# GRU and top-2 mixture on one core: GpSimd sums the last chunk's four blocks, in buffers that the slabs held

## The chip, the cores and the metric

The kernel runs on one core of a Trainium2 chip. The metric is device time in microseconds of one execution, taken as the median over several runs. A profile of one execution goes with it. The engines are named as the profile names them: PE (matrix multiply), DVE (vector), ACT (scalar), POOL (GpSimd) and SP (here only an issuer of DMAs).

## The reference

The input `x` has 16 sequences of 256 steps with 512 features, all float32. A GRU runs over the steps from the state `cond_2048`. Each of its 4096 hidden rows then goes through a mixture of eight low-rank experts, of which the router takes the best two, and the result is added to `x`.

```python
def cell(h, x):
    gi = x @ W_ih + b_ih
    gh = h @ W_hh + b_hh
    ...
    n = jnp.tanh(i_n + r * h_n)
    h_new = (1.0 - z) * n + z * h
...
router_logits = x / norm @ router_w
routing_weights = jax.nn.softmax(router_logits.astype(jnp.float32), axis=-1)
rw, selected_experts = jax.lax.top_k(routing_weights, TOP_K)
rw = rw / jnp.sum(rw, axis=-1, keepdims=True)
...
for e in range(N_EXPERTS):
    out = out + combine[:, e, None] * (x @ Wa[e] @ Wb[e])
...
x = x + _L0_ffn_ref(_L0_cond_ref(cond_2048, x, ...), ...)
```

In the mixture, `x` stands for the GRU's hidden rows.

## The kernel before

The GRU is sequential, so the 256 steps set the length of the program. They are grouped into 32 blocks of eight steps; one block is 128 rows (16 sequences by 8 steps), which is one row for each partition. The mixture's work is put between the steps, while the GRU goes on.

The first 29 blocks go through the mixture in four chunks of 7, 11, 7 and 4 blocks (`CHUNKS`, L24). For each chunk, `Route` finds the two experts of each row. `Chunk` then gives each row two slots in a list that is sorted by expert, and scatters the rows to it in DRAM. `Slab` takes the list 128 rows at a time: it loads them (tile `xg`), copies one expert's two matrices into tiles of its own (`wag` and `wbg`, by POOL, L677 and L681), multiplies, and stores the result `y` to the DRAM buffer `y_slots` (L722). When a chunk's last slab is done, one `Combine` is begun for each block:

- `load` issues the load of the block's `x` rows on SP (`xr`, L746) and two indirect DMAs on POOL, which gather the first and the second expert's rows from `y_slots` (`yg`, L750).
- `add(0)` and `add(1)` each do `xr = y * w + xr` in one DVE instruction over 128 rows and 512 columns (L764); `w` is a column with one weight per row.
- After `add(1)`, SP issues the store of `xr` to the output (L768).

The last three blocks (29, 30 and 31) are too late for a chunk. `Moe` sends each of them through all eight experts, weighted by the combine weights. `prep` and `route` make the logits. `soft1` to `soft3` make the weights: the norm on POOL (L815), then on DVE the softmax and `top2`, which begins with a small memset by POOL (tile `pr`, L307) that DVE's maximum (L312) needs. Then PE multiplies by the first matrices (L833), DVE scales by the weights (`a`, L845), PE transposes (L854), ACT copies back (L860), and PE multiplies by the second matrices (L870). `load` fetches the block's `x` rows on SP (L797), `store` adds PE's result to them on DVE (L880), and SP issues the store of the block (L881).

A planner in the Python program sets the order. Each of these objects is an agent with a list of `Piece`s. After each GRU step, and in a loop behind the last step, `choose` walks through the agents by rank and takes every piece whose gap has passed and whose buffers (`takes`, counted in `room`) are free. The two tile names "xr" and "yg" have three and two buffers; "xg" and "wg" have four each. Combines have rank 8 and stand ahead of the last block's `Moe`, which has rank 41. What is picked in a round is written to the engines in that order, and `keep_order` at the end holds each engine to the order in which its instructions were written. So SP, which issues almost all DMAs, issues them strictly in that order, and waits at one whose data are not ready.

In the last stage, behind the last GRU step, the remaining work is: the last slabs of the last chunk, the four combines of that chunk (they are called A, B, C and D below, in their order), and `Moe` of blocks 30 and 31.

Of the kernel before, what the change touches and what calls it, by code (L numbers as in the profile page):

```python
# [8 lines left out]
FP = mybir.dt.float32  # L9
# [8 lines left out]
ALU = mybir.AluOpType  # L18
# [3 lines left out]
P = 128  # L22
TS = 8
CHUNKS = [7, 11, 7, 4]  # L24
# [20 lines left out]
def gru_moe_kernel(  # L45
# [47 lines left out]
    pe, dve, act, pool, sp = nc.tensor, nc.vector, nc.scalar, nc.gpsimd, nc.sync  # L93
    B, T, D = x.shape
    E, _, R = wa.shape
# [13 lines left out]
    slb = ctx.enter_context(tc.tile_pool(name="slb", bufs=4))  # L109
# [6 lines left out]
    moe = ctx.enter_context(tc.tile_pool(name="moe", bufs=2))  # L116
# [29 lines left out]
    for side, src in enumerate((b_ih, b_hh)):  # L146
        for g in (0, 2, 1):
            tag = ("xg", "wbg")[side]
# [173 lines left out]
    class Piece:  # L322
# [4 lines left out]
        def __init__(self, gap=1, cost=0.0, pe=(), then=(), takes="", gives=""):  # L327
            self.gap, self.cost = gap, cost
            self.pe, self.then = list(pe), list(then)
            self.takes, self.gives = takes.split(), gives.split()  # L330
# [16 lines left out]
    class Early:  # L347
# [5 lines left out]
        def load(self):  # L353
            m = self.m
            if self.x is not None:
                return
            self.x = slb.tile([P, D], FP, tag="yg1", bufs=2, name=f"xe_{m}")
            for j in range(NJ):
                for s in range(2):
                    p0 = 32 * j + 16 * s  # L360
                    sp.dma_start(
                        self.x[p0 : p0 + B, 0:P],
                        x[:, 2 * m + s, j * P : (j + 1) * P],
                    )
# [40 lines left out]
        def plan(self):  # L405
            pieces = [
                Piece(then=[("load",)], takes="early"),
                Piece(gap=2, then=[("turn",)], takes="at"),
            ] + [
                Piece(gap=0, cost=c, pe=[("into", what, q)])  # L410
                for what, c in (("rn", 0.43), ("z", 0.22))
                for q in range(NQ)
            ] + [Piece(then=[("store",)], gives="early")]
            pieces[2].gap, pieces[2].takes = 1, ["ps"]
            pieces[9].then, pieces[9].gives = [("keep",)], ["ps", "at"]
            return pieces
# [320 lines left out]
    class Combine:  # L737


        def __init__(self, i, chunk, k):  # L740
            self.i, self.chunk, self.k = i, chunk, k

        def load(self):
            i, ch = self.i, self.chunk
            self.xr = moe.tile([P, D], FP, tag="xr", bufs=3, name=f"xr_{i}")
            sp.dma_start(self.xr, x[:, i * TS : (i + 1) * TS, :])  # L746
            self.y = []
            for n, ix in enumerate(ch.idx):
                y = slb.tile([P, D], FP, tag=f"yg{n}", bufs=2, name=f"yg_{i}_{n}")
                pool.indirect_dma_start(  # L750
                    out=y[:, :],
                    out_offset=None,
                    in_=ch.y[:, :],
                    in_offset=bass.IndirectOffsetOnAxis(
                        ap=ix[:, self.k : self.k + 1], axis=0
                    ),
                    bounds_check=ch.n_slabs * P - 1,
                    oob_is_err=False,
                )
                self.y.append(y)  # L760

        def add(self, n):
            i, k, o = self.i, self.k, self.xr
            dve.scalar_tensor_tensor(  # L764
                o, self.y[n], self.chunk.w[n][:, k : k + 1], o, ALU.mult, ALU.add
            )
            if n:
                sp.dma_start(out[:, i * TS : (i + 1) * TS, :], o)  # L768

        def plan(self):  # L770
            return [
                Piece(then=[("load",)], takes="xr yg"),
                Piece(gap=3, then=[("add", 0)], takes="turn", gives="turn"),
                Piece(then=[("add", 1)], takes="turn", gives="turn xr yg"),
            ]


# [230 lines left out]
    room = dict(ROOM)  # L1008
# [104 lines left out]
    for i in range(NB):  # L1113
# [26 lines left out]
        if i < n_sparse:  # L1140
            ch = chunks[-1]
            k = i - (ends[ch.c] // TS - ch.k)
# [55 lines left out]
```

## Time and profile before

| | us |
|---|---|
| median of three runs | 1357.65 |
| lowest and highest | 1355.23, 1357.68 |
| the profiled execution, its own time | 1356.92 |
| its span, first to last instruction | 1355.1 |
| PE busy | 1292.5 (95% of the span) |
| DVE busy | 736.2 (54%) |
| ACT busy | 392.1 (29%) |
| POOL busy | 284.4 (21%) |

The granted TensorE clock was 0.994 over the span. How to read the rows: a row of a group gives the line of the program, the engine, the operation, the tiles it writes and reads, the shape, how often it ran, its busy time in total and the mean time of one, and what ended the idle time before it. A row of the timeline gives the start, the duration, and then the same; in square brackets stands the idle time before it and who ended it. "SPq" is SP's queue: such a row is the issue of a DMA, not its transfer. In the chain of waits, a row "DMA" is the time from an issue to the point where the data had landed.

### The profile page before, as it was taken

What the parts mean: (1) busy time and instruction counts of PE and PEld (TensorE: products, weight loads), DVE (VectorE), ACT (ScalarE), POOL (GpSimd) and SP (SyncE); (2) the same over time, 40 slices, a digit from 0 to 9 for tenths busy, and PEclk for the clock granted to TensorE, in tenths of its full rate; (3) what the DMA queues carried; (4) which work ended last, traced back from release to release, by engine and by line L of the source; (5) the groups of instructions that cost most, each with busy time, mean ns of one, the idle gap of its engine ahead of it and who ended that gap; (6) DMA issues with size and microseconds to landing.
All of it is one profiled execution on the core that took longest, in us unless ns stands there. A gap on an engine that the chain in (4) does not pass through costs nothing. (4 is left out here: it accounts for less than half of the span.)

```text
span 1355.1 us, 68450 instructions
## 1 busy us (share of the span) xinstructions
PE 1292.5 (95%) x30378; PEld 929.7 (69%) x30378; DVE 736.2 (54%) x2678; ACT 392.1 (29%) x1354; POOL 284.4 (21%) x504
## 2 busy tenths in 40 slices
PE   6899999999999999999999999999998999989996
PEld 3577777776677777777776677777766787768752
DVE  1455555555455555555555456555565555665543
ACT  1223222322233333233332233333332333323220
POOL 2000000102221000000003323221133033353452
PEclk8999999999999999999999999999999999999998
DMA  8532322223322111122124535553345345664685
GB/s 200 143 122 97 99 91 90 91 61 130 95 72 61 55 56 56 41 59 57 50 65 132 182 90 158 151 148 101 95 142 167 103 135 168 174 199 129 199 253 167
DMA packets 149477, 158.67 MB, mean 117 GB/s; under 512 B 22646, under 2 KB 103606, under 8 KB 149180
## 3 DMA queue, kind: packets, MB, share of 16 engines
q1 hardware_dynamic: 139760, 123.83, 31.1%
q0 software_dynamic: 9280, 30.42, 7.1%
q8 instruction: 238, 3.90, 1.2%
q14 instruction: 59, 0.48, 0.1%
q10 hardware_dynamic: 140, 0.05, 0.0%
HBM read 84.21 MB, written 69.99 MB: 114 GB/s over the span
## 5 line engine op out<-in xcount | busy, mean ns | idle before, releaser
L921 PE MATMUL rn<-whh,hist 128*32 128x256 f32 x8160 | 507.8, 381 | 19.9 <-DVE hist L966 14.1
L921 PEld LDWEIGHTS rn<-whh,hist 128*32 128x32 f32 x8160 | 264.0, 109 | 198.5 <-DVE hist L966 48.3
L269 PE MATMUL rn<-wih,xT 128*32 128x256 f32 x3712 | 307.3, 382 | 9.3 <-DMA wih<-in_L_cond_W_ih_dram 5.5
L931 PE MATMUL z<-whh,hist 128*32 128x128 f32 x8160 | 289.9, 273 | 6.4 <-issue 5.8
L954 DVE SCALAR_TENSOR_TENSOR n<-r,rn 128x128 f32<-128x128 f32 x256 | 73.5, 287 | 397.6 <-ACT r L947 393.0
L931 PEld LDWEIGHTS z<-whh,hist 128*32 128x32 f32 x8160 | 247.3, 110 | 51.7 <-issue 13.5
L277 PE MATMUL z<-wih,xT 128*32 128x128 f32 x3712 | 209.0, 274 | 5.5 <-ACT z L952 3.3
L947 ACT ACTIVATE r<-rn 128x128 f32<-128x128 f32 x256 | 70.9, 277 | 460.7 <-PE rn L921 448.8
L277 PEld LDWEIGHTS z<-wih,xT 128*32 128x32 f32 x3712 | 138.5, 110 | 77.3 <-issue 6.3
L269 PEld LDWEIGHTS rn<-wih,xT 128*32 128x32 f32 x3712 | 126.7, 110 | 19.0 <-issue 13.1
L959 DVE SCALAR_TENSOR_TENSOR zh<-z,h 128x128 f32<-128x128 f32 x255 | 77.8, 305 | 86.0 <-ACT z L952 83.1
L952 ACT ACTIVATE z<-z 128x128 f32<-128x128 f32 x256 | 71.0, 277 | 170.7 <-PE z L931 144.7
L698 PE MATMUL at_ps<-xgT,wag 128*32 128x128 f32 x2752 | 110.1, 273 | 3.9 <-issue 3.5
L629 POOL TENSOR_TENSOR nrm<-ss,half 128x1 f32<-128x1 f32 x29 | 16.2, 559 | 435.5 <-ACT ht L627 408.2
L713 PE MATMUL y_ps<-wbg,at 128*32 128x256 f32 x1376 | 103.2, 380 | 1.0 <-issue 0.9
L698 PEld LDWEIGHTS at_ps<-xgT,wag 128*32 128x32 f32 x2752 | 87.6, 110 | 13.9 <-issue 10.2
L966 DVE STREAM_TRANSPOSE hist<-rows 128x128 f32<-128x128 f32 x256 | 79.7, 311 | 8.7
L974 DVE STREAM_TRANSPOSE h<-hist 128x128 f32<-128x128 f32 x256 | 79.7, 311 | 8.7
L681 POOL COPY wbg<-wb_sb 128x512 f32 x86 | 56.3, 655 | 126.0 <-PE y_ps L713 125.9
L963 DVE SCALAR_TENSOR_TENSOR rows<-zh,m 128x128 f32<-128x128 f32 x256 | 75.9, 297 | 8.9
L721 ACT COPY y<-y_ps 128x512 f32<-128x512 f32 x86 | 50.1, 583 | 101.9 <-PE y_ps L713 88.3
L961 DVE SCALAR_TENSOR_TENSOR m<-z,n 128x128 f32<-128x128 f32 x256 | 77.7, 303 | 2.4 <-ACT n L956 1.4
(136 smaller groups left out, 1072.4 us busy)
## 6 DMA issues: line engine op xcount, KB each, us to landing
xg<-x_slots SPq DMA_DIRECT2D x344, 64.0 KB
y_slots<-y SPq DMA_DIRECT2D x86, 256.0 KB
ht<-H SPq DMA_DIRECT2D x58, 256.0 KB
x_slots<-zero SPq DMA_DIRECT2D x50, 256.0 KB
x<-in_x_dram SPq DMA_DIRECT2D x256, 32.0 KB
xr<-in_x_dram SPq DMA_DIRECT2D x32, 256.0 KB
out_dram<-xr SPq DMA_DIRECT2D x32, 256.0 KB
H<-rows SPq DMA_DIRECT2D x232, 32.0 KB
```

Of the source, the lines that this page charges most:

```text
L269: pe.matmul(rn[32 * j : 32 * j + 32, 0 : 3 * P].rearrange("p (g d) -> p g d", g=3)[:, 0:3:2, :], lhsT=xts[m][:, q, :], rhs=w[:, 0:3:2, j, ...
L277: ins = pe.matmul(zb[32 * j : 32 * j + 32, 0:P], lhsT=xts[m][:, q, :], rhs=w[:, 1, j, :], start=False, stop=(q == NQ - 1), skip_group_chec ...
L698: pe.matmul(self.ps[c32, 0:P], lhsT=self.wa[:, q, c32], rhs=self.xt[:, q, :], start=(q == 0), stop=(q == NQ - 1),)
L713: pe.matmul(self.ps[c32, half], lhsT=self.at[:, c32], rhs=self.wb[:, half], start=True, stop=True,)
L921: pe.matmul(rn[32 * j : 32 * j + 32, 0 : 2 * P].rearrange("p (g d) -> p g d", g=2), lhsT=hT[:, q, :], rhs=w(q, j)[:, 0:3:2, :], start=Fals ...
L931: pe.matmul(zb[32 * j : 32 * j + 32, 0:P], lhsT=hT[:, q, :], rhs=w(q, j)[:, 1, :], start=False, stop=(q == NQ - 1), skip_group_check=True,)
L954: dve.scalar_tensor_tensor(n, r, 1.0, rn[:, P : 2 * P], ALU.add, ALU.mult)
L959: dve.scalar_tensor_tensor(zh, z, 1.0, hrow, ALU.add, ALU.mult)
L961: dve.scalar_tensor_tensor(m, z, 1.0, n, ALU.subtract, ALU.mult)
L963: dve.scalar_tensor_tensor(hn, zh, 0.5, m, ALU.mult, ALU.subtract)
L966: dve.transpose(hist[:, t, :, lo : lo + 32], hn.rearrange("p (q c) -> p q c", q=NQ))
L974: dve.transpose(hrow.rearrange("p (q c) -> p q c", q=NQ), hT)
```

## The change

For the last chunk alone (`self.last`), `Combine` changes in three ways. The `x` rows of its four blocks are loaded into buffers of the tile name "xg" and the gathered rows into buffers of "wag" and "wbg". These have four buffers each, and the slabs are through with them by then; so the plan takes and gives room "xg wg" in place of "xr yg". And the sum is done by POOL, in two instructions in place of one: a multiplication of the gathered rows by the weight column, in place, and an addition to the `x` rows.

```diff
         def load(self):
             i, ch = self.i, self.chunk
-            self.xr = moe.tile([P, D], FP, tag="xr", bufs=3, name=f"xr_{i}")
+            if self.last:
+                self.xr = slb.tile([P, D], FP, tag="xg", name=f"xr_{i}")
+            else:
+                self.xr = moe.tile([P, D], FP, tag="xr", bufs=3, name=f"xr_{i}")
             sp.dma_start(self.xr, x[:, i * TS : (i + 1) * TS, :])
             self.y = []
             for n, ix in enumerate(ch.idx):
-                y = slb.tile([P, D], FP, tag=f"yg{n}", bufs=2, name=f"yg_{i}_{n}")
+                tag, bufs = (("wag", "wbg")[n], 4) if self.last else (f"yg{n}", 2)
+                y = slb.tile([P, D], FP, tag=tag, bufs=bufs, name=f"yg_{i}_{n}")
                 pool.indirect_dma_start(
...
         def add(self, n):
             i, k, o = self.i, self.k, self.xr
-            dve.scalar_tensor_tensor(
-                o, self.y[n], self.chunk.w[n][:, k : k + 1], o, ALU.mult, ALU.add
-            )
+
+            if self.last:
+                w = self.chunk.w[n][:, k : k + 1]
+                pool.tensor_scalar_mul(self.y[n], self.y[n], w)
+                pool.tensor_add(o, o, self.y[n])
+            else:
+                dve.scalar_tensor_tensor(
+                    o, self.y[n], self.chunk.w[n][:, k : k + 1], o, ALU.mult, ALU.add
+                )
             if n:
                 sp.dma_start(out[:, i * TS : (i + 1) * TS, :], o)
 
         def plan(self):
+            room = "xg wg" if self.last else "xr yg"
             return [
-                Piece(then=[("load",)], takes="xr yg"),
+                Piece(then=[("load",)], takes=room),
                 Piece(gap=3, then=[("add", 0)], takes="turn", gives="turn"),
-                Piece(then=[("add", 1)], takes="turn", gives="turn xr yg"),
+                Piece(then=[("add", 1)], takes="turn", gives=f"turn {room}"),
             ]
```

`self.last` is set in `__init__` to `chunk.c == len(CHUNKS) - 1`.

More of the change, by code (lines that the diff above doesn't have):

```diff
@@ L741, in __init__ @@
             self.i, self.chunk, self.k = i, chunk, k
+            self.last = chunk.c == len(CHUNKS) - 1
         def load(self):
             i, ch = self.i, self.chunk
-            self.xr = moe.tile([P, D], FP, tag="xr", bufs=3, name=f"xr_{i}")
+            if self.last:
+                self.xr = slb.tile([P, D], FP, tag="xg", name=f"xr_{i}")
+            else:
+                self.xr = moe.tile([P, D], FP, tag="xr", bufs=3, name=f"xr_{i}")
             sp.dma_start(self.xr, x[:, i * TS : (i + 1) * TS, :])
```

## The prediction

> **What bounds the kernel now.** The page comes first: PE is busy 95% of the span, because the GRU runs to the last step. But the change touches only the last chunk's combines, and these run after the GRU. So what counts is the stage behind the last step, and there the table of stages shows another picture. Its columns are: window, length, then busy time of PE, weight loads, DVE, ACT and POOL, the granted clock, DMA share and GB/s.
>
> ```profile
> 1330.00:1340.00 10.00, 9.80 (x92) 3.81 (x88) 6.34 (x21) 1.57 (x4) 3.82 (x6) 1.00 0.49 145
> 1340.00:1350.00 10.00, 5.11 (x48) 1.30 (x40) 2.94 (x5) 0.00 (x0) 0.90 (x1) 0.91 0.60 170
> 1350.00:1356.00 6.00, 0.00 (x0) 0.00 (x0) 0.58 (x1) 0.00 (x0) 0.00 (x0) 0.50 0.42 124
> ```
>
> PE is through at 1345.1, and in the last fifteen microseconds no engine is busy for most of the time. The chain of waits says what is:
>
> ```profile
> 1338.08 5.29 DMA out_dram<-xr
> ...
> 1343.39 4.27 DMA xr<-in_x_dram
> ...
> 1347.78 0.06 DVE xr L880
> ...
> 1349.83 0.75 DVE xr L764
> ```
>
> Read it backward. The last DVE sum ends at 1350.58, and the span ends 4.52 us later (1355.1): that is the last store and the end of the program. Ahead of it DVE works off a pile (L880, then three L764) that all began when the x rows of block 31 landed at 1347.66. Their load (L797) was issued only at 1343.39, as its buffer, one of three "xr", came free when a combine's store had landed. PE's result had been ready since 1345.1. So the bound is the supply of "xr" buffers and SP's order, and the span has about 2.7 us (1347.8 less 1345.1) of waiting past PE in it.
>
> That waiting is all that freeing buffers could win. The timeline of POOL, over the same stretch, is where the new work goes:
>
> ```profile
> 1323.47 1.07 POOL L750 DMA_INDIRECT yg<-y_slots,ihi  x1 [2.41 <-DMA y_slots<-y]
> ...
> 1327.46 1.00 POOL L750 DMA_INDIRECT yg<-y_slots,ilo  x1 [0.30 <-issue]
> 1330.17 0.57 POOL L815 TENSOR_TENSOR nrm<-lg,half 128x1 f32<-128x1 f32 x1 [1.71 <-DVE lg L813]
> 1330.71 0.09 POOL L307 MEMSET pr<- 128x6 f32 x1
> 1332.78 1.04 POOL L750 DMA_INDIRECT yg<-y_slots,ihi  x1 [1.97 <-DVE rs L309]
> ```
>
> **What the change moves.** The two programs, laid side by side, issue the same instructions in the same order on PE and ACT, and on all engines up to the first combine of the last chunk. The differences are these. DVE loses its last eight L764. SP's last ten issues change from
>
> ```
> before: store 30, load B, store A, store B, load C, load D, load 31, store 31, store C, store D
> after:  store 30, load B, load C, load D, store A, store B, store C, store D, load 31, store 31
> ```
>
> (L881, L746, L768, L797 by their names above). POOL's order becomes: gathers A and B, norm (L815), gathers C, multiply and add of A's first half, gathers D, memset (L307), then seven more pairs of multiply and add. So three things happen: load 31 gets a free buffer, but stands behind all four combine stores; each of those waits for POOL; and the memset that block 31's top-2 needs stands behind four gathers and one pair.
>
> **The price of a pair.** The add is two-input, 128x512. The nearest rows on POOL, with counts and means:
>
> ```profile
> L681 POOL COPY wbg<-wb_sb 128x512 f32 x86 | 56.3, 655 | 126.0 <-PE y_ps L713 125.9
> L393 POOL TENSOR_TENSOR ge<-ge,bias 128x256 f32<-128x256 f32 x12 | 8.8, 732 | 0.0
> L392 POOL TENSOR_TENSOR ge<-ge,bias 128x128 f32<-128x128 f32 x12 | 5.5, 458 | 78.1 <-ACT ge L389 77.8
> L792 POOL TENSOR_TENSOR sq<-hc 128x512 f32<-128x512 f32 x3 | 3.2, 1059 | 2.4 <-issue 2.2
> ```
>
> L792 has the size but reads one tile twice: 1.06 us. L392 and L393 are true in-place adds of two tiles: 0.274 us more for 128 more columns, so 0.73 + 2 x 0.274 = 1.28 us at 512. The Trainium skill ("GPSIMD Engine Reference", section 3.1, Elementwise — side-by-side cycle accounting) states about 2.6 cycles per element for a two-input operation; at its 1.2 GHz an estimate from that page is 512 x 2.6 / 1.2 = 1.11 us before dispatch. I take 1.2. Eight adds by the row of L792 or by the extrapolation differ by 8 x 0.22 = 1.8 us, which goes into the range.
>
> The multiply by a weight column is one-input. The trace has no such operation on POOL. From below it is a copy of the size, 0.655 us (L681); from above the two-input price, 1.28. The same page (section 4.1, Engine selection) says one-input operations run at roughly line rate, and speaks against moving two-input ones from VectorE at all. I take 0.70, near the copy, as a copy too is one-input. The add reads what the multiply wrote and waits for its semaphore, which no row on POOL shows apart; POOL's independent rows follow one another with none of it, so from 0 to 0.2, and I take 0.1. A pair is 0.70 + 0.1 + 1.2 = 2.0 us. DVE needed 0.75 (L764).
>
> **The sum on POOL**, in the profiled execution's own time. Up to the norm nothing changes: it ends at 1330.74. Gathers C need no freed buffer: two issues with a period of 1.30 (1324.85 to 1326.16 above), from 1330.95 to 1333.3. Pair A-first to 1335.3; its gathers were issued at 1323.5, and DVE used the same data at 1331.74 before. Gathers D to 1337.8, memset to 1337.95. Seven pairs, 14.0: POOL ends at 1352.0. The later gathers are at least 8 us ahead of their pairs, so their landing costs nothing. I charge nothing for POOL and DVE disturbing each other: DVE has nothing to do from about 1340.5 (the second L845) until L880.
>
> **The sum behind it.** Store D is issued at 1352.05 and takes SP's usual 0.6. Load 31 goes out at 1352.7. For its landing the chain has 4.27, with loads C and D and a gather still moving. At the end of the span SP issued the last store at 1350.58 and saw it landed at 1353.25 (after a wait of 2.1): 2.7 us behind two other stores. The Trainium skill ("DMA: Bandwidth & Descriptors", section Anatomy of one DMA — SWDGE path) fits 2.0 us plus bytes over 436 GB/s, for 256 KB an estimate of 2.6. Here one store runs beside the load; I take 3.0 (between ends of 2.6 and 4.27): landed at 1355.7. With 4.27 the end would come 1.3 later. Then L880 needs 0.12 + 0.69, to 1356.5, and the 4.5 us from the last DVE sum to the end are as before: **1361.0**, which is 5.9 us past 1355.1. The freed buffer wins nothing, as it was buffer and queue together that held the load: taking away the one, the other holds it 9.3 us longer (1352.7 against 1343.39).
>
> **What stays covered.** The late memset moves DVE's L312 from 1332.94 to 1338.0. From L312 to the end of the weights is 1.12 us, then L845 to 1339.9, and 1.44 from the first transpose to L870, which runs 7.07: PE ends at 1348.5 instead of 1345.1. That is 3.4 us later, hidden by the load that lands at 1355.7; were that load early, it would be the next bound. The eight L764 taken off DVE (6 us) win nothing for the same reason; what of them was on the path is the three behind L880, some 2.1 us, already counted in that L880 is now the last.
>
> **The time.** The profiled execution took 1356.92; plus 5.9 is 1362.8. The runs shown have their median 0.7 above it (1357.65), which gives 1363.5. I say 1363.2. About 0.2% (2.7 us) is what a measurement of this kernel can tell from no change.
>
> **Rivals.**
>
> 1. The multiply on POOL costs like the two-input rows or more (1.28 us, from the upper bound), adds 1.28: a pair is 2.66 us, POOL ends 8 x 0.66 = 5.3 us later, and the time is 1368.5. For it: a weight column has to be fetched per partition. Against: the copy's row, and the rule of one input. Chance 0.2.
> 2. Not slower: POOL is quick enough that load 31 no longer decides. Then the late memset does, and PE ends at 1348.5, L880 at 1349.3, the span at 1353.8, that is 1355.6 in time (1.3 faster, within 0.2%). It decides if the load lands by 1348.5, so if POOL is through by about 1344.8: seven pairs in 6.8 us, under 1.0 each. Against it: L792's 1.06 alone is more than that. Chance 0.04, with 0.01 in it for a gain past 0.2%.
> 3. The change doesn't reorder SP as said, or load 31 is issued ahead of the stores: the same time as in 2, and no more than 0.01, as the order on the queue is fixed in the program.
> 4. Cheap pairs all the same (0.65 + 1.06, no gap: 1.71) and a landing of 2.6: POOL ends 2.3 earlier, the load 0.4: 1360.5. Chance 0.2. The likeliest case, about 1361.5 to 1365.5, has 0.55.
>
> The range, 1360.0 to 1368.3, takes in cases 1 (most of it) and 4. Faster 0.01 (out of 2), same 0.04 (the rest of 2, and 3), slower 0.95.
>
> **What would show it.** In the profile after, the chain of waits should end in: POOL's adds, store D's issue, DMA of `xr` from the input, DVE L880's sum, DMA to the output. SP should show one load (L797's line) after four stores. POOL's groups should have eight multiplies near 0.7 us and eight adds near 1.2. L312 should start near 1338, and PE should end near 1348.5, some 7 us ahead of the last DVE sum. I am wrong if a POOL pair is below 1 us, or if PE's last result ends later than the load lands.

## The result, and the profile after

The changed kernel is slower: 1372.9 us (median of six runs, 1370.1 to 1375.5) against 1356.8 for the kernel before (six runs). The ratio is 1.011, with a 95% interval of 1.0098 to 1.0122. That is 16.1 us more, where 5.9 were forecast; 1372.9 lies above the range, which ended at 1368.3. The profiled execution took 1372.6, with a span of 1370.8.

Times of whole executions drift by several microseconds, and seven experiments (the last seven rows of the table of tails) ran on a second chip, where the kernel before has its median at 1302, about 4% lower. So each ratio is against executions of the kernel before on the same chip, and for the mechanism one length is used that is free of the GRU: the **tail**, from the start of block 31's norm (L815 before, L828 after) to the end of the span, in one profiled execution of each kernel. Before it is 1355.1 - 1330.2 = 24.9 us, after 1370.8 - 1330.6 = 40.2. No tail of these two kernels was taken on the second chip. POOL's multiplies and adds cost the same there (1.56 to 1.58 and 1.26 to 1.27 us in the run with the memset early), so tails are compared across the chips.

The table of stages after, with the columns as before (length, busy time of PE, weight loads, DVE, ACT, POOL, granted clock, DMA share, GB/s):

```profile
1330.00:1340.00 10.00, 7.07 (x84) 2.39 (x69) 1.51 (x8) 0.39 (x2) 6.66 (x7) 0.99 0.59 181
1340.00:1350.00 10.00, 6.98 (x48) 3.00 (x52) 2.29 (x9) 1.17 (x2) 9.74 (x9) 0.66 0.29 80
1350.00:1360.00 10.00, 2.86 (x28) 0.61 (x20) 0.00 (x0) 0.00 (x0) 9.70 (x7) 0.85 0.20 52
```

POOL, nearly idle behind 1340 in the kernel before, is now busy from 1340 to 1360 almost without a break, and once PE is through (1352.9) no other engine is, until DVE's last sum at 1365.5. The chain of waits, from its end:

```profile
1357.14 1.26 POOL xr L774
1358.41 1.54 POOL yg L773
...
1361.32 0.54 SPq L780
...
1361.91 3.49 DMA xr<-in_x_dram
...
1365.53 0.69 DVE xr L893
```

It is the forecast's chain, link for link: POOL's last pair (its add, for which the chain has a row of POOL's queue in the place of the dots, runs from 1360.03 to 1361.29), the issue of store D, only then load 31, its landing, DVE's last sum. SP's rows show the queue: the four stores as one row of 17.9 us, in which SP does little but wait, and the load behind them.

```profile
1343.95 17.90 SPq L780 DMA_DIRECT2D out_dram<-xr  x4
1361.91 0.59 SPq L810 DMA_DIRECT2D xr<-in_x_dram  x1
```

What was mis-sized is in POOL's groups (busy time in total, mean of one in ns):

```profile
L774 POOL TENSOR_TENSOR xr<-xr,yg 128x512 f32<-128x512 f32 x8 | 10.1, 1266 | 0.7
L773 POOL TENSOR_SCALAR yg<-yg,whi 128x512 f32<-128x512 f32 x4 | 6.3, 1569 | 0.0
L773 POOL TENSOR_SCALAR yg<-yg,wlo 128x512 f32<-128x512 f32 x4 | 6.3, 1569 | 0.0
```

The add costs 1.27 us, near the 1.2 that was taken. The one-input multiply costs 1.57 us, where 0.70 was taken: it is dearer than the two-input add.

### The profile page after: what moved, and what is told of

It reads as the page before. It is cut to its first block, busy times and chain, and to the rows that moved or that the text cites. A ratio compares the mean times of both kernels' runs of the same rounds, so it can differ in the third digit from the quotient of the medians.

```text
span 1370.8 us, 68447 instructions
## 1 busy us (share of the span) xinstructions
PE 1291.9 (94%) x30378; PEld 934.7 (68%) x30378; DVE 729.6 (53%) x2670; ACT 392.7 (29%) x1354; POOL 308.3 (22%) x520
## 4 chain that ended last, share of the span: by engine, by line
PE 84%; DVE 4%; DMA 3%; issue 2%; another core or an unknown queue 2%; POOL 2%; ACT 2%; SPq 0%; POOLq 0%; ACTq 0%; DVEq 0%
PE rn L934 33%; PE z L944 16%; PE rn L269 13%; PE z L277 6%; PE y_ps L713 5%; PE at_ps L698 5%; PE gi L377 2%; DMA whh<-in_L_cond_W_hh_dram 1%; PE a_ps L846 1%; PE rt L341 1%; POOL yg L773 1%; DVE m L974 1%; DMA wih<-in_L_cond_W_ih_dram 1%; DVE rows L976 1%
## 5 line engine op out<-in xcount | busy, mean ns | idle before, releaser
L969 ACT ACTIVATE n<-n 128x128 f32<-128x128 f32 x256 | 77.3, 302 | 4.1 <-DVE n L968 3.5
```

Source lines behind the costliest of these rows:

```text
L969: act.activation(n, n, AF.Tanh)
```

## The experiments

All are made from the changed kernel unless said otherwise. The tails of all runs come first (us); "more than before" is the difference of the medians, for scale.

| kernel | tail | ratio to before, 95% interval | more than before |
|---|---|---|---|
| before | 24.9 | 1 | |
| changed kernel | 40.2 | 1.011 (1.0098 to 1.0122) | +16.1 |
| load 31 ahead of the stores | 36.0 | 1.0088 (1.0058 to 1.0118) | +11.7 |
| buffers alone, sum on DVE | 26.1 | 1.0023 (1.0006 to 1.0040) | +2.5 |
| POOL alone, old buffers | 34.6 | 1.0073 (1.0054 to 1.0092) | +9.3 |
| ACT multiplies, POOL adds | 29.4 | 1.0028 (1.0010 to 1.0045) | +4.4 |
| POOL multiplies by a number | 39.7 | 1.0132 (1.0092 to 1.0172) | +16.1 |
| POOL multiplies two-input | 35.6 | 1.0068 (1.0035 to 1.0102) | +8.9 |
| memset early | 40.1 | 1.0112 (1.0074 to 1.0149) | +13.9 |
| one more gather | 41.0 | 1.0142 (1.0121 to 1.0162) | +18.7 |
| buffers, DVE, load 31 early | 27.2 | 1.0006 (0.9994 to 1.0017) | +1.5 |
| buffers, DVE, memset early | 22.3 | 0.9974 (0.9963 to 0.9984) | -3.4 |
| buffers, DVE, both early | 21.3 | 0.9975 (0.9959 to 0.9992) | -4.9 |

**Load 31 ahead of the stores.**

```diff
-            pieces[14].then, pieces[14].takes = [("load",)], ["xr"]
+            k = 4 if self.i == NB - 1 else 14
+            pieces[k].then, pieces[k].takes = [("load",)] + pieces[k].then, pieces[k].takes + ["xr"]
```

> As the changed kernel, but the x rows of block 31 are loaded ahead of the four combine stores on SP; nothing else moves. Theory (POOL's rate and SP's order together): POOL still ends its last add at 1361.3 of the span, but only the last store follows it, so the 5 us of load and sum behind it go: span about 1365.9, time about 1368 (changed kernel 1372.9, before 1356.8). Rival 1 (PE was made late by the memset and its clock fell to 0.66, and that sets the end): no gain, about 1373. Rival 2 (the queue is the whole cause): back to before, about 1357.

Measured: the span is 1367.4 with the norm 0.85 later than in the changed kernel, so the tail is 36.0: 4.2 us won. The expectation, counted the same way, was 1365.9 - 1330.6 = 35.3. So PE's lateness (rival 1) does not set the end. Nor is the queue the whole cause (rival 2): with load 31 out of it the kernel still ends 11 us later than before, on POOL's last add.

**The buffers alone.**

```diff
-                pool.tensor_scalar_mul(self.y[n], self.y[n], w)
-                pool.tensor_add(o, o, self.y[n])
+                dve.scalar_tensor_tensor(o, self.y[n], w, o, ALU.mult, ALU.add)
```

> The buffers of the changed kernel, but the sum on DVE in one instruction as before; SP's order as in the changed kernel (four stores, then load 31). Theory (POOL's slow pair is the cause, the buffers and the queue cost nothing by themselves): gathers C and D end near 1338, the memset behind them, so DVE's sums end near 1345.5, load 31 is issued at 1346 and lands at 1349.6: span about 1355, time within 2 us of before. Rival (the queue order costs by itself): the load is held as long as in the changed kernel, over 1362. Rival (the freed buffers win their 2.7 us): about 1354.

Measured: span 1354.9, tail 26.1. So 14.1 of the 15.3 us that the tail grew come from POOL's sum, the queue that it holds up included. But the reason given for the span was wrong in one link. DVE's rows, then PE's:

```profile
1342.97 0.75 DVE L773 SCALAR_TENSOR_TENSOR xr<-yg,wlo,xr 128x512 f32<-128x512 f32 x1
1349.57 0.69 DVE L892 TENSOR_TENSOR xr<-o_ps,xr 128x512 f32<-128x512 f32 x1 [5.85 <-PE o_ps L882]
```

```profile
1338.29 0.65 PE L866 MATMUL aT_ps<-ident,a 128*128 128x128 f32 x4 [3.04 <-DVE a L857]
1340.21 1.12 PE L866 MATMUL aT_ps<-ident,a 128*128 128x128 f32 x4 [1.27 <-DVE a L857]
1341.26 8.23 PE L882 MATMUL o_ps<-wb_sb,aT 128*32 128x512 f32 x64
```

The last sum waits for PE, not for load 31. PE is late by the memset that stands behind the gathers, and then it is slow: its last 64 matmuls take 8.23 us, where they took 7.07 in the kernel before. The runs with the memset or the load moved, below, take this apart.

**POOL alone, in the old buffers.** The three uses of `self.last` that choose buffers and room are taken back; the sum stays on POOL.

> The sum on POOL as in the changed kernel, but in the buffers of before (three xr, two and two yg). SP's order becomes: stores A and B, loads C, D and 31, store 31, stores C and D. Theory: seven of eight pairs at 2.9 us still run one after another with gathers C and D between them, POOL ends near 1360, and the last thing is store D: span about 1364.5, time about 1366.5, so 6 us less than the changed kernel although it has fewer buffers. Rival (the buffers help POOL's sum, by earlier gathers): slower than the changed kernel, over 1374.

Measured: span 1363.7, tail 34.6, so 5.6 us shorter than the changed kernel's. The freed buffers do not help POOL's sum; they cost. With the old ones, the loads C, D and 31 go out after store B and ahead of stores C and D, and load 31 is at 1344.3:

```profile
1335.58 6.39 SPq L780 DMA_DIRECT2D out_dram<-xr  x2
1342.06 1.23 SPq L751 DMA_DIRECT2D xr<-in_x_dram  x2
1344.30 0.54 SPq L810 DMA_DIRECT2D xr<-in_x_dram  x1
1351.64 0.59 SPq L894 DMA_DIRECT2D out_dram<-xr  x1
1353.38 6.30 SPq L780 DMA_DIRECT2D out_dram<-xr  x2
```

With the new ones nothing in the planner holds the four stores back, and they go ahead of it. The load's place alone is 4.2 of the 5.6 us, as the run with load 31 moved shows.

**ACT multiplies.**

```diff
-                pool.tensor_scalar_mul(self.y[n], self.y[n], w)
+                act.mul(self.y[n], self.y[n], w)
```

> As the changed kernel, but ACT multiplies by the weight column (8 instructions, 0.59 us each by ACT's copies of the size) and POOL only adds. Theory (the end follows POOL's time one for one, through load 31): eight multiplies of 1.57 us leave POOL, it ends near 1348.5, load 31 goes out at 1349.1, span about 1358, time about 1360. Rival 1 (PE's delay sets the end): no change, 1373. Rival 2 (ACT's own order holds the adds up, as its copies for block 31 wait for PE among the multiplies): between 1363 and 1370.

Measured: span 1360.8, where 1358 was expected, tail 29.4, time 4.4 us over before. The end follows POOL's time, but rival 2 took 2.2 us of it (and ACT's multiply took 0.71, not 0.59): ACT's copies for block 31 stand among its multiplies and wait for PE, so POOL's adds pause.

```profile
1340.10 5.06 POOL L774 TENSOR_TENSOR xr<-xr,yg 128x512 f32<-128x512 f32 x4
1347.37 3.86 POOL L774 TENSOR_TENSOR xr<-xr,yg 128x512 f32<-128x512 f32 x3 [2.21 <-ACT yg L773]
```

**What makes the multiply dear.** Two runs replace it on POOL. One multiplies by a number and leaves the weights out, so that its output is not the reference's; the other uses a two-input multiplication with the column repeated:

```diff
-                pool.tensor_scalar_mul(self.y[n], self.y[n], w)
+                pool.tensor_scalar_mul(self.y[n], self.y[n], 0.5)
```

> As the changed kernel, but POOL multiplies the gathered rows by the number 0.5 in place of the weight column (the weights are left out). Theory A (the weight column, an operand fetched per partition, makes the multiply dear): it falls from 1.57 us to about a copy's 0.65, POOL ends 8 x 0.92 = 7.4 us earlier, span about 1363.5. Theory B (the operation itself costs 1.57 us on POOL): no change, span about 1370.8.

```diff
-                pool.tensor_scalar_mul(self.y[n], self.y[n], w)
+                pool.tensor_tensor(
+                    self.y[n], self.y[n], w.broadcast_to([P, D]), ALU.mult
+                )
```

> As the changed kernel, but POOL's multiply is written as a two-input operation, the weight column repeated over the 512 columns. If the two-input price holds (1.27 us, as the add): POOL ends 8 x 0.3 = 2.4 us earlier, span about 1368.5. If a repeated column costs as much as the operation with a scalar column: 1.57 us, span about 1370.8.

POOL's groups, the first from the run with a number, the other two from the two-input run:

```profile
L773 POOL TENSOR_SCALAR yg<-yg 128x512 f32<-128x512 f32 x8 | 12.0, 1497 | 0.0
```

```profile
L776 POOL TENSOR_TENSOR xr<-xr,yg 128x512 f32<-128x512 f32 x8 | 10.1, 1267 | 0.6
L773 POOL TENSOR_TENSOR yg<-yg,whi 128x512 f32<-128x512 f32 x4 | 4.2, 1043 | 0.0
L773 POOL TENSOR_TENSOR yg<-yg,wlo 128x512 f32<-128x512 f32 x4 | 4.2, 1040 | 0.0
```

The column accounts for 0.07 us; the operation itself costs 1.50. Theory B holds. Why it is so dear, no run shows. The same product as a two-input operation costs 1.04, less than either expectation had: like the square of one tile in the kernel before (1.06), not like an add of two tiles (1.27). The tail shrinks by 4.6, of which 8 x 0.53 = 4.2 is the multiply: the price of this one operation does move the end.

**The memset early.** For block 31 it is issued in `soft1`, behind the norm, in place of `top2`.

> As the changed kernel, but the memset that block 31's top-2 needs is issued right behind the norm, ahead of gathers C. Theory (the memset's lateness is covered by POOL's sums): PE ends 7 us earlier, near 1346, with its matmuls back at 7.1 us in all, and the time stays at that of the changed kernel within 1.5 us. Rival (PE's lateness is what costs): about 7 us less, near 1366.

Measured: tail 40.1 against 40.2, though PE ends 14.9 us after the norm's start and not 22.3. The ratio, 1.0112, is that of the changed kernel. So PE's lateness is covered, as the prediction had it. PE's rows, here and then in the changed kernel:

```profile
1280.33 7.07 PE L888 MATMUL o_ps<-wb_sb,aT 128*32 128x512 f32 x64
```

```profile
1343.02 1.97 PE L867 MATMUL aT_ps<-ident,a 128*128 128x128 f32 x8 [5.95 <-DVE a L858]
1344.92 7.94 PE L883 MATMUL o_ps<-wb_sb,aT 128*32 128x512 f32 x64
```

**Buffers and DVE, with the memset, the load, or both moved.** Each is made from the buffers-alone kernel with one or both of the edits above.

> Buffers of the changed kernel, the sum on DVE, load 31 ahead of the four stores, the memset still behind gathers C and D. The tail is counted from the start of block 31's norm to the end of the span: 24.9 us before, 26.1 with buffers and DVE alone, 21.3 with memset and load moved as well. Theory (with the sum on DVE, the late memset holds PE and PE's end decides): moving the load alone wins nothing, tail 26 us. Rival (the load behind the stores decides): 21 to 23 us.

> Buffers of the changed kernel, the sum on DVE, the memset right behind the norm, load 31 still behind the four stores. Theory: DVE's last sum comes 13 us after the norm's start, the load goes out at 13.6, its rows land at 17.2, and 0.8 + 4.5 follow: tail 22.5 us, most of what both moves won. Rival (the load behind the stores decides as much as in the changed kernel): 25 us or more.

> The buffers of the changed kernel, the sum on DVE as before, the memset behind the norm, and load 31 ahead of the four stores. Theory: nothing is left in front of PE's end at 1345 (in before's own time), L880's sum runs at once, and the span ends 0.8 + 4.5 later, near 1350.5: 4.5 us less than before, which is 0.3%. Rival (one of the three is not the bound any more and something else takes its place, as the sums of C and D ahead of L880 on DVE waiting for gathers): within 1.5 us of before.

Measured tails: 27.2 with the load alone, 22.3 with the memset alone, 21.3 with both, each within 1.2 us of what was expected (26, 22.5, and 1350.5 - 1330.2 = 20.3). The memset's place is worth 27.2 - 21.3 = 5.9 us with the load early. Of these, 2.3 are PE's last 64 matmuls, which take 9.36 us with the memset late and 7.07 with it early; most of the rest is the later start. The load's place is worth 1.0 (22.3 - 21.3), and only once the memset is out of the way: with the memset late, the tail is longer by 1.1 with the load early (27.2 against 26.1), which is again PE's last matmuls (9.36 against 8.23). The version with both is 3.6 us shorter in its tail than the kernel before; its ratio is 0.9975 (0.9959 to 0.9992), that of the memset alone 0.9974 (0.9963 to 0.9984). So these two are quicker than the kernel before, by a quarter of a percent: little, but neither interval reaches 1. In the chain of the version with both, what is left is PE's work and the sum behind it:

```profile
1276.71 7.05 PE o_ps L887 x64
1283.76 0.02 issue
1283.78 0.69 DVE xr L897
```

**The late gather.** In the changed kernel the second gather of C waits 2 us:

```profile
1331.34 1.04 POOL L756 DMA_INDIRECT yg<-y_slots,ihi  x1 [0.19 <-issue]
1334.37 1.02 POOL L756 DMA_INDIRECT yg<-y_slots,ilo  x1 [1.99 <-DMA xr<-in_x_dram]
```

The name of a load in the brackets is an inference of the profile; the data that this gather needs had long been there. The edit issues the second gather of the first chunk's first block twice.

> As the changed kernel, with one gather of the first chunk issued twice, so one more indirect DMA some 800 us ahead of the tail. In the changed kernel and in those made from it the second gather of C starts some 2 us late; it is the sixth of the last chunk and the 114th indirect DMA of the program. Theory 1 (it is the count: something happens at the 114th): the late one is now the first gather of C, the fifth of the chunk, and the sixth follows at the usual 0.3. Theory 2 (it is the number in flight in this stage): still the sixth.

```profile
1280.20 1.05 POOL L757 DMA_INDIRECT yg<-y_slots,ihi  x1 [2.72 <-issue]
1281.56 1.01 POOL L757 DMA_INDIRECT yg<-y_slots,ilo  x1 [0.30 <-DMA xr<-in_x_dram]
```

With one more gather long before, the wait moves one gather forward: it goes with the count of indirect DMAs since the program's start, at the 114th, and not with the number in flight in this stage. What happens at that count, no run shows. The second row's bracket shows again how little the named DMA means: the 0.30 there is the usual distance.

## Why the prediction was right or wrong

**Direction and mechanism: right.** Load 31 behind four stores, each behind POOL; the load's landing, DVE's last sum and the last store behind that. The chain after shows it, and moving the load alone takes 4.2 us out of the tail.

**Size: wrong, by the multiply on POOL.** It was taken at 0.70 us and measured 1.57. The forecast's tail was 1361.0 - 1330.2 = 30.8 us; measured 40.2. The 9.4 us between them are made up so:

| term | forecast | measured | difference |
|---|---|---|---|
| eight pairs | 8 x 2.0 | 8 x 2.89 (start to start) | 7.1 |
| gathers C, from the norm's end | 2.56 | 4.24 | 1.7 |
| load 31, issue to DVE's start | 3.1 | 3.6 | 0.5 |
| the rest | | | 0.1 |

- *The multiply's price* is the step that failed: 8 x 0.87 = 7.0 us of the missing 9.4. It was bounded from below by a copy (0.655) and from above by the two-input price (1.28), and taken near the copy as the row with one input. Both ends were of other operations. An operation with a scalar on POOL is a kind of its own here: 1.50 to 1.57 us, outside the bounds. The Trainium skill ("GPSIMD Engine Reference", section 4.1, Engine selection) has one-input operations at roughly line rate; the trace's copy (0.655) fits that, its multiply (1.57) doesn't, and the measurement decides. Rival 1 had the direction right, but with 1.28 as its price it stopped at 1368.5.
- *The add's price* was right within 0.07: the extrapolation from the adds of two tiles (1.28) meets 1.27, and the square (1.06), which reads one tile twice, misleads. The Trainium skill's 2.6 cycles per element ("GPSIMD Engine Reference", section 3.1, Elementwise — side-by-side cycle accounting) is not what was low: from 128 to 256 columns the adds of two tiles rise by 0.274 us, by our estimate 2.6 cycles at that page's 1.2 GHz, and from 256 to 512 by 0.534, which is 2.5. What 1.11 leaves out is a fixed part, by the same rows about 0.18 us (0.458 - 0.274); 1.2 had room for 0.09.
- *The wait of the add for the multiply* (0.1) was right: the add starts 1.65 us after the multiply does, which ends at 1.57.
- *Gathers C*: the period of 1.30 was right for seven of eight. The late one was there before too, at 1337.25, though its buffer had come free when DVE's sum ended at 1335.51; I read "issue" in its bracket as no cause and passed over it.
- *The landing*: 3.49 where 3.0 was taken, inside the bounds (2.6 to 4.27). The lower bound was the page's fit for DMAs that GpSimd issues; load 31 is issued by SP, so the fit was not made for it.
- *What stays covered* was right: PE late, no cost, as the run with the memset early shows. PE's end came later than said (1352.9, not 1348.5): 3.1 us because the memset itself was late, 1.3 us because its transposes and matmuls took longer after the idle stretch, which was not in the sum (0.5 and 0.9 us).
- *The sentence that the freed buffers win nothing* holds for the changed kernel, and says too little: with POOL's sum they cost 5.6 us (40.2 against 34.6), and with DVE's sum and the memset's place put right they win 2.6 us (24.9 against 22.3), or 3.6 with the load early too.

**The time on record**: tail 9.4 us longer, and the rest of the 9.7 us (1372.9 against 1363.2) is the base.

## What to carry to other kernels

An operation without a row in the trace is not bounded by its neighbours: a scalar multiply on GpSimd cost more than both the copy and the add that were to enclose it, so a range on such a term has to reach well past the rows, above all when it is multiplied by eight. When an agent's buffers are freed, look at what its own waits had kept back in a shared queue: here the old buffers held two slow stores behind a load that the end depended on. And look for the small instruction that a block of work is put in front of: a memset of 0.1 us behind four gathers was worth 5.9 us, once the cover was gone, and 2.3 of these were PE's slower matmuls after the pause.

## What the runs showed of the hardware

- **Some DVE instructions are held by POOL's two-input operations, and were not by its scalar ones.** Two small DVE instructions (L318, L319) ran at their usual length in the changed kernel, beside a POOL multiply. Where POOL was adding (ACT multiplies), they ended with POOL's adds. First the changed kernel, then the run with ACT:

```profile
1341.74 0.16 DVE L318 TENSOR_SCALAR mask_b<-rp 128x8 f32<-128x8 f32 x1
1341.94 0.23 DVE L319 SCALAR_TENSOR_TENSOR cb_b<-pr,s,mask_b 128x8 f32<-128x8 f32 x1
```

```profile
1340.88 1.76 DVE L318 TENSOR_SCALAR mask_b<-rp 128x8 f32<-128x8 f32 x1
1342.67 1.29 DVE L319 SCALAR_TENSOR_TENSOR cb_b<-pr,s,mask_b 128x8 f32<-128x8 f32 x1
```

  Not every DVE instruction is held: L312 to L317, beside the first of these adds, kept their lengths (0.09 to 0.20 us). In the run with POOL alone, a DVE instruction of 0.23 us (L310) took 1.22 and ended with POOL's add. The Trainium skill ("SBUF — State Buffer", section Who interferes with whom) has a read port that the two engines share and one holds for a whole instruction; the stretched rows fit that, and the multiply that stretches nothing is not in it. The prediction charged nothing for this, and the trace before could have warned: a sum on DVE that began 0.24 us after POOL's square took 1.41 us and not 0.75.

```profile
1319.96 1.10 POOL L792 TENSOR_TENSOR sq<-hc 128x512 f32<-128x512 f32 x1 [2.19 <-issue]
1320.20 1.41 DVE L764 SCALAR_TENSOR_TENSOR xr<-yg,wlo,xr 128x512 f32<-128x512 f32 x1
```

  For the changed kernel the zero was right, in part by luck: L318 and L319 happened to lie beside a multiply. Had they been held, PE's end would have come some 2.7 us later by the rows above, and still well ahead of load 31's landing (1352.9 against 1365.4).

- **PE's clock after a pause.** After 5.95 us of idle time PE's 64 matmuls took 7.94 us and not 7.07, and the granted clock of that stage was 0.66 (0.99 in the stage before it). With pauses of 1.2 us or less (memset early, both early) they took 7.07. With pauses of 3.04 and 1.27 in a row they took 8.23 (buffers alone) and 9.36 (load 31 early, sum on DVE); there the four transposes right behind the 3.04 still ran at full speed (0.65), and only those behind the second pause were slow (1.12). The Trainium skill ("TensorE: Matmul & The Clock Gate", Part 1) puts the drop to half rate at about 3.4 us of idle time; the runs fit that roughly, but here two shorter pauses in a row were enough.

- **The 114th indirect DMA of the program is late.** The idle time of POOL before it is 1.95 to 1.99 us in most of these runs (about 0.3 or less is usual behind another gather or the norm), 1.25 with POOL alone and 2.72 with one more gather.
